# Three PSUM banks each for two kinds of score tiles in the first attention of a two-layer block

## The chip, the cores and the metric

The kernel runs on one core of a Trainium2 chip. A core has a matrix engine (TensorE, PE in the profile, with its weight loads as PEld), a vector engine (DVE), a scalar engine (ACT), a general engine (GpSimd, POOL) and SyncE (SP), which here issues the DMA transfers. Each engine works through its own instructions in order; semaphores tie them together. Matrix products are written to PSUM[...].

The metric is the device time of one execution in microseconds (us).

## The reference

Two layers run over x, 16 sequences of 256 tokens with 128 features. Each layer normalises, scales and shifts by a modulation, applies a mixing block, adds its gated output, and does the same with a second block. The change touches the first block alone: full attention with 16 heads of 8 features.

```python
q = (hidden_states @ Wq.T + bq).reshape(b, s, HEADS, HEAD_DIM)
k = (hidden_states @ Wk.T + bk).reshape(b, s, HEADS, HEAD_DIM)
v = (hidden_states @ Wv.T + bv).reshape(b, s, HEADS, HEAD_DIM)
q = q * SCALE
scores = jnp.einsum('bqhd,bkhd->bhqk', q, k)
probs = jax.nn.softmax(scores.astype(jnp.float32), axis=-1)
out = jnp.einsum('bhqk,bkhd->bqhd', probs, v).reshape(b, s, d)
return out @ Wo.T + bo
```

The blocks after it are a six-deep local transformer (attention in windows of 32 tokens and a gated feed-forward), a state-space scan, and a linear layer with a low-rank correction.

## The kernel before, in words

The whole program is one launch: `full_attention`, then `local_transformer`, then `state_space` (L1343 to L1362). Activations stay in SBUF as `xT`, features on the partitions.

`full_attention` (L132) works on groups `g` of two sequences and on units `u` of one sequence. Scores are computed twice. The first time (`scores`, L272, tile `s`, queries on the partitions) they serve only to find each row's maximum: `maxima` (L290) reduces them on DVE (L296). `turn` (L298) transposes the negated maxima (`pm`), copies them (`nT`), and writes them by DMA (L311) into spare rows of the query tile `qm`, with a row of ones in the key tile `kT`. The second time (`exponents`, L314, tile `sT`, keys on the partitions) the product so contains score minus maximum; `exponentials` (L334) apply exp on ACT (L337) into `e`; `gather` (L353) multiplies with the values into `po`, with the row sums beside them (L370). `after` (L379) inverts the sums (`pr`, reciprocal on DVE, product on POOL) and applies the output projection (`py`).

A head group has 32 rows, so the array holds four row groups. `pair(k, h)` (L340) handles two of them. For step `k + 6` it issues the first scores of row groups 2h and 2h+1, for step `k` the exponents of the other two row groups, then the second half of the first scores, then the two maxima and the two exponentials. Every `s` and every `sT` tile is [128, 2, 256] f32.

The order on each engine is written out: the loop at L417 over `k` runs under `manual_schedule` and calls `pair(k, 0)`, a slot, half of `gather(k - 1)`, a slot, `pair(k, 1)`, the other half of `gather(k - 1)`, a slot. A slot takes one piece of other work from a list `todo`: the next group's load, normalisation and projections (`before`, L197, with `xin`, `px`, the transposes at L119, called `ln2` in the code, `pq`, `qm`, `pk`), the values (`pv`), `turn` and `after`. For `k` from -6 to -1 there are first scores only; for `k` from 58 on, exponents and gather only.

PSUM is divided into tile pools. Those of the first attention:

```python
sp = ctx.enter_context(tc.tile_pool(name="a0S", bufs=2, space=PSUM))
tp = ctx.enter_context(tc.tile_pool(name="a0T", bufs=4, space=PSUM))
ps = ctx.enter_context(tc.tile_pool(name="a0p", bufs=1, space=PSUM))
op = ctx.enter_context(tc.tile_pool(name="a0o", bufs=1, space=PSUM))
```

A pool hands out its buffers in turn; the first write to a tile waits until the buffer's previous tile has been read. `scores` takes its two `s` tiles at once (L279), when it issues the first halves. `exponents` takes one `sT` after the other (L323). All pieces of other work share the one buffer of `ps`; `po` has the one of `op`. Pools of the later stages are opened after this function has closed its own.

## Time and profile before

| | |
|---|---|
| Median of 3 runs | 4388.13 us (4386.72 to 4397.31) |
| Profiled execution, its own time | 4388.87 us |
| Its span, first to last instruction | 4386.8 us |
| Busy: PE, DVE, ACT, POOL | 94%, 79%, 58%, 59% |
| First attention, first `s` to last `gather` | about 35 to 473 us |
| Local transformer | about 523 to 3815 us |
| Mean of one reduction of `s` (L296) | 688 ns |
| Mean of one exponential (L337) | 595 ns |

Each row of the order of time gives the start in us from the start of the span, the length of the merged row in us, engine, line, operation, output and inputs, shapes and count; in brackets stands the idle time of that engine before it and who ended it. In a row of waits stand the waiting engine and line, the one waited for, then us in total, times, and the longest. A matrix product in f32 appears as two records, each with its own weight load. PE's rows overlap, since products of different row groups run side by side.

### The profile page before, as it was taken

Reading aid. Unit: us, or ns where it says so; the run is one execution under the profiler, and the core shown is the slowest. Engines: PE = TensorE matmul, PEld = TensorE weight load, DVE = VectorE, ACT = ScalarE, POOL = GpSimd, SP = SyncE. Lnnn points to the kernel's source line nnn. Section 1 sums busy time; section 2 is a strip of 40 time slices with the busy share of each in tenths; the row PEclk is TensorE's granted clock in tenths of the full one; section 3 lists DMA queues with packets and bytes.
Section 4 is the critical chain, followed back from the end, with each engine's and each line's share of the span. In section 5 each row is a group of like instructions: output and inputs, shape, how many; then the busy total and the mean of one; then the engine's idle time right before and its main releaser. Section 6 shows DMA issues by size and latency. Waiting matters only on the chain.

```text
span 4386.8 us, 97989 instructions
## 1 busy us (share of the span) xinstructions
PE 4104.9 (94%) x42544; PEld 2447.8 (56%) x42544; DVE 3481.1 (79%) x4876; ACT 2527.3 (58%) x3299; POOL 2568.6 (59%) x1552
## 2 busy tenths in 40 slices
PE   6888589999999999999999999999999999779998
PEld 4444355665656656556566565565655556445554
DVE  3554488888888888888888888888888988569997
ACT  2454455555555555555555555555555555379995
POOL 1111276666666666666666666666666666258887
PEclk9999799999999999999999999999999999989999
DMA  0000100000000000000000000000000000033433
GB/s 19 7 7 4 54 2 2 2 2 22 7 1 2 2 22 6 2 2 2 22 6 2 1 2 22 6 2 1 2 1 2 2 1 2 12 98 104 115 104 85
DMA packets 59562, 83.01 MB, mean 19 GB/s; under 512 B 5800, under 2 KB 31228, under 8 KB 58364
## 3 DMA queue, kind: packets, MB, share of 16 engines
q1 hardware_dynamic: 59132, 76.74, 6.2%
q8 instruction: 335, 5.49, 0.5%
q14 instruction: 95, 0.78, 0.1%
HBM read 73.84 MB, written 2.62 MB: 17 GB/s over the span
## 4 chain that ended last, share of the span: by engine, by line
PE 57%; DVE 24%; ACT 4%; issue 2%; POOL 1%; SPq 0%; ACTq 0%; DVEq 0%; POOLq 0%; DMA 0%
PE pq L566 13%; PE py L743 11%; PE pa L724 10%; DVE w L589 4%; DVE u L578 4%; PE fp L807 4%; ACT sq L573 3%; PE fy L829 3%; PE s L669 3%; PE pt L629 3%; PE y L1241 3%; DVE ss L600 3%; PE db L1225 2%; DVE s L1231 2%; DVE pp L687 1%
## 5 line engine op out<-in xcount | busy, mean ns | idle before, releaser
L606 POOL TENSOR_TENSOR u<-u,w 128x1024 f32<-128x1024 f32 x384 | 902.0, 2360 | 321.1 <-DVE w L589 182.1
L620 POOL TENSOR_TENSOR u<-u,r 128x1024 f32<-128x1024 f32 x384 | 720.3, 1902 | 175.9 <-DVE r L616 175.9
L573 ACT ACTIVATE sq<-pq 128x1024 f32<-128x1024 f32 x384 | 388.4, 1024 | 664.8 <-PE pq L566 331.1
L706 POOL TENSOR_TENSOR pp<-pp,sm 128x1024 f32<-128x1024 f32 x192 | 367.1, 1912 | 619.1 <-DVE sm L702 619.1
L566 PE MATMUL pq<-wqk,F 128*128 128x512 f32 x1536 | 722.4, 598 | 4.0 <-ACT sq L573 1.4
L743 PE MATMUL py<-at,wvo 128*128 128x256 f32 x3072 | 712.2, 382 | 2.3 <-ACT at L734 2.3
L724 PE MATMUL pa<-pT,xw 32*128 32x512 f32 x3072 | 651.6, 616 | 30.3 <-ACT sq L573 29.2
L743 PEld LDWEIGHTS py<-at,wvo 128*128 128x128 f32 x3072 | 568.3, 190 | 134.2 <-issue 47.6
L578 DVE TENSOR_TENSOR u<-pq,cosl 128x1024 f32<-128x1024 f32 x384 | 463.2, 1206 | 190.5 <-ACT sq L573 190.5
L589 DVE TENSOR_TENSOR w<-pq,sinl 128x512 f32<-128x512 f32 x768 | 491.3, 681 | 80.5 <-PE pq L566 80.1
L734 ACT COPY at<-pa 128x1024 f32<-128x1024 f32 x384 | 383.4, 1012 | 275.3 <-PE pa L724 272.4
L600 DVE TENSOR_REDUCE ss<-sq 128x16 f32<-128x1024 f32 x384 | 455.8, 1198 | 2.6 <-ACT sq L573 1.1
L566 PEld LDWEIGHTS pq<-wqk,F 128*128 128x128 f32 x1536 | 273.5, 191 | 275.9 <-issue 244.8
L629 PEld LDWEIGHTS pt<-ident,u 128*128 128x128 f32 x3072 | 348.4, 142 | 123.9 <-issue 73.7
L629 PE MATMUL pt<-ident,u 128*128 128x128 f32 x3072 | 398.2, 275 | 20.5 <-POOL u L620 19.7
L724 PEld LDWEIGHTS pa<-pT,xw 32*128 32x128 f32 x3072 | 233.0, 184 | 291.0 <-issue 182.3
L1231 DVE TENSOR_TENSOR_SCAN s<-da,db 128x512 f32<-128x512 f32 x256 | 301.1, 1208 | 24.3 <-PE db L1225 9.9
L296 DVE TENSOR_REDUCE mx<-s 128x2 f32<-128x512 f32 x256 | 165.2, 688 | 194.0 <-PE sT L324 170.0
L807 PE MATMUL fp<-hT,w 128*128 128x512 f32 (+1 forms) x576 | 268.1, 602 | 39.8 <-DVE w L589 38.0
L669 PEld LDWEIGHTS s<-kT,qT 64*32 64x32 f32 x24576 | 254.1, 105 | 82.1 <-issue 81.1
L669 PE MATMUL s<-kT,qT 64*32 64x64 f32 x24576 | 285.1, 225 | 0.5 <-ACT kT L637 0.5
L1241 PE MATMUL y<-hc,ident 128*128 128x512 f32 x512 | 244.2, 604 | 16.1 <-POOL hc L1235 14.3
(214 smaller groups left out, 6291.1 us busy)
## 6 DMA issues: line engine op xcount, KB each, us to landing
btd<-bc SPq DMA_DIRECT2D x72, 512.0 KB
bte<-bc SPq DMA_DIRECT2D x56, 256.0 KB
wqk<-in_Wqk SPq DMA_DIRECT2D x6, 1024.0 KB
wv<-in_LWvT SPq DMA_DIRECT2D x6, 512.0 KB
wo<-in_Wo SPq DMA_DIRECT2D x6, 512.0 KB
xin<-in_x SPq DMA_DIRECT2D x8, 256.0 KB
out<-ot SPq DMA_DIRECT2D x8, 256.0 KB
w<-in_W SPq DMA_DIRECT2D x6, 341.0 KB
```

The lines of the kernel that those rows point to most:

```text
L566: nc.tensor.matmul(q.p[:, x], self.F[:, g.b0 + b, o : o + P], g.l.wqk[:, k, x, :], start=True, stop=True)
L573: self.c.nc.scalar.activation(q.sq, q.p, AF.Square)
L578: self.c.nc.vector.tensor_tensor(q.u.rearrange("p h x d -> p x h d"), q.p, g.l.cosl[:, t, k].unsqueeze(2).to_broadcast([P, 2, HEADS, DH // ...
L589: self.c.nc.vector.tensor_tensor(q.w[:, :, x], q.p[:, 1 - x], g.l.sinl[:, t, k, x, :].unsqueeze(1).to_broadcast([P, HEADS, DH // 2]), ALU. ...
L600: self.c.nc.vector.tensor_reduce(g.ss[b][:, t, k, :], q.sq.rearrange("p x h d -> p h x d"), AX.XY, ALU.add)
L606: self.c.nc.gpsimd.tensor_tensor(q.u, q.u, q.w, ALU.add)
L620: self.c.nc.gpsimd.tensor_tensor(uf, uf, g.r[b][:, t, k, :].unsqueeze(2).to_broadcast([P, HEADS, DH]), ALU.mult)
L629: self.c.nc.tensor.transpose(q.pt[:, j, :], uf[:, j * P : (j + 1) * P], self.c.ident)
L669: nc.tensor.matmul(s[qs, e, j, :], qT[es, j, qs], kT[es, j, ks : ks + 2 * W], start=False, stop=True, skip_group_check=True,)
L724: self.c.nc.tensor.matmul(pa[:, x, :], g.xw[b, t][qs, k, :], g.pT[b, t][qs, k, :], start=(k == 0), stop=(k == 1),)
L743: self.c.nc.tensor.matmul(g.py[b], g.l.wvo[:, h, :], self.at[:, h, :], start=(h == 0), stop=(h == HEADS - 1),)
L807: self.c.nc.tensor.matmul(p[0:n, x, :], g.l.w1[:, w : w + n], g.hT, start=True, stop=True)
```

## The change

The pool of the first scores `s` gets three buffers instead of two, that of the transposed scores `sT` three instead of four. Nothing else differs: the same instructions stand in the same order on every engine.

```diff
-        sp = ctx.enter_context(tc.tile_pool(name="a0S", bufs=2, space=PSUM))
-        tp = ctx.enter_context(tc.tile_pool(name="a0T", bufs=4, space=PSUM))
+        sp = ctx.enter_context(tc.tile_pool(name="a0S", bufs=3, space=PSUM))
+        tp = ctx.enter_context(tc.tile_pool(name="a0T", bufs=3, space=PSUM))
```

## The prediction

> **What bounds the kernel now.** I read the page first: TensorE is busy 94% of a span of 4386.8 us, and the chain of work that ended last does not reach back before the end of the first attention (about 473 us). So that stage was read from its own views. The busy time by stage says how long it is (columns: length, busy us of PE, its weight loads, DVE, ACT, POOL, granted clock, DMA share, GB/s):

> ```profile
> 30.00:93.00 63.00, 51.09 (x188) 29.43 (x188) 23.24 (x43) 14.65 (x24) 4.16 (x5) 1.00 0.00 1
> 93.00:446.00 353.00, 301.69 (x2589) 157.67 (x2588) 179.40 (x299) 174.49 (x327) 52.00 (x57) 0.97 0.02 6
> 446.00:473.00 27.00, 25.50 (x185) 8.86 (x184) 1.76 (x1) 15.23 (x29) 2.71 (x3) 1.00 0.00 1
> ```

> No engine is full: DVE and ACT are half idle, and PE stands still for 51 of 353 us. The waits from 93 to 446 us say for whom (us in total, times, longest):

> ```profile
> PEld s L282 <- DVE mx L296: 61.9, 119, 0.8
> ...
> PE s L282 <- DVE mx L296: 15.2, 53, 0.3
> PE py L395 <- POOL o L390: 15.0, 14, 1.1
> ```

> The first scores `s` wait for their bank to be read by the maxima. The order of time shows how one step (a pair of `s` tiles, which I call pair) runs (start, length, engine):

> ```profile
> 208.77 1.08 PE L282 MATMUL s<-kT,qm 32*128 32x256 f32 x3 [0.27 <-DVE mx L296]
> ...
> 209.37 0.18 PEld L282 LDWEIGHTS s<-kT,qm 32*128 32x128 f32 x1 [0.30 <-DVE mx L296]
> ...
> 210.43 0.64 PE L370 MATMUL po<-e,vp 128*32 128x256 f32 x8
> 210.53 1.08 ACT L337 ACTIVATE e<-sT 128x512 f32<-128x512 f32 x2 [1.51 <-PE sT L324]
> 210.62 1.29 DVE L296 TENSOR_REDUCE mx<-s 128x2 f32<-128x512 f32 x2 [0.82 <-PE sT L324]
> ...
> 211.37 1.08 PE L282 MATMUL s<-kT,qm 32*128 32x256 f32 x3 [0.29 <-DVE mx L296]
> 211.97 0.18 PEld L282 LDWEIGHTS s<-kT,qm 32*128 32x128 f32 x1 [0.31 <-DVE mx L296]
> ```

> Call X the start of a pair's second `s` (209.37). From it `gather` starts at X+1.06, the exponentials at X+1.16, the maxima at X+1.25. One reduction takes 0.69 us, the two 1.29. The next first `s` starts at 211.37, 0.06 after the first reduction has ended (210.62+0.69), the next second `s` at 211.97, 0.06 after the second. So a pair takes X to X = 1.25+1.29+0.06 = 2.60 us. It is a circle through PE, DVE and one bank each, in which neither engine is full.

> [...] the trace does not show banks, but its waits fit one bank for each tile. [...] here four row groups run side by side and the reader sets the pace, as above. [...] the clock is 0.51 from 178.9 to 182.3 us after an idle of 2.48 us.

> **The change part by part.** Nothing is added to or removed from any engine; only who waits for whom.

> *Three banks for `s`.* A pair takes two of three, in turn: (0,1), (2,0), (1,2). Its first `s` falls on the second bank of the pair before last, long free. Its second `s` falls on the first bank of the pair before, read after the first reduction. So X to X becomes 1.25+0.69+0.06 = 2.00 us, 0.60 less. PE could go at X+1.06+0.48 (gather: eight records, four side by side, two deep at 0.24) = X+1.54, so the bank still sets the pace; DVE is busy 1.29 of 2.00.

> This is won only where both `s` wait. The view has that 53 times from 93 to 446 us. From 38 to 90 us the order of time shows 8 more such pairs (2.85 us each, since weight loads take 0.28 there instead of 0.18, though the stage's clock is given as 1.00; the stagger of 0.60 is the same); two others there are followed by transposes that wait for POOL. 61 in all. Pairs with other work between them wait for something else and give nothing:

> - `pr`, `py`, `pm`, `pv`: fixed chains from X. The reciprocal starts after the second reduction (X+2.46), 1.75, then 1.27 on POOL, and `py` starts at X+5.67; then `pm`, ACT's copy, `pv`. Nothing there waits for an `s` bank alone.
> - `pq`, three ACT copies, one DVE copy, `pk`: PE idle 2.48, six times; fixed.
> - `px`, six times, one pair after a waiting one: it waits for its transfer.

> ```profile
> 198.24 2.27 SPq L311 DMA_DIRECT2D qm<-nT  x4
> ...
> 200.63 0.37 SPq L202 DMA_DIRECT2D xin<-in_x  x1
> ...
> 203.31 0.42 PEld L210 LDWEIGHTS px<-ident,xin 128*128 128x128 f32 x4 [0.58 <-DMA xin<-in_x]
> ```

> SP issues it only after four `nT` transfers, which start when ACT's copy ends; it lands 5.1 us after that copy whatever PE does. A pair that ends 0.60 earlier only makes `px` wait longer. So 6 of the 61 give nothing: 55 x 0.60 = 33.0. Where DVE's four statistics follow the reductions (0.86 us, end X+3.32), the next reduction is wanted at X+3.25: minus 0.07, six times = -0.4. At 90.6 us one pair has PE free 0.3 before its bank: +0.3. The pair after `px` waits for the second reduction alone and starts 0.2 sooner (6 x 0.2 = 1.2); that after the `ln2` transposes 0.38 sooner, of which the wait of `pq` for `hT` leaves 0.3 (6 x 0.3 = 1.8). Sum: 35.9.

> *Three banks for `sT` instead of four.* This adds a wait: the second `sT` of a pair takes the bank of the first `sT` of the pair before, read by its first exponential. In a plain pair that ends at X+1.16+0.60, +0.06 = X+1.82. The `sT` stands in PE's order behind the second `s`, at X+2.00 now. So it is covered, by 0.18. If that cover were gone, the second half of `s`, `gather`, and so both the maxima and the exponentials behind it would start later by what ACT is late. In the fixed chains the next pair comes at X+2.5 or later. ACT's other copies (0.37 to 0.59 each) mostly run after the exponentials of their pair or are done before the next. I take 0; bounds: no gain is possible from fewer banks, and the loss is at most 0.3 for each of the 55 (PE waiting for both exponentials, X+2.25+0.06 = 2.31), 17 us.

> At the end (446 to 473 us) there are `sT` and `gather` alone, one pair in 1.63 us:

> ```profile
> 454.81 1.13 PE L324 MATMUL sT<-qm,kT 32*128 32x512 f32 x4
> ...
> 455.97 1.08 ACT L337 ACTIVATE e<-sT 128x512 f32<-128x512 f32 x2 [0.54 <-PE sT L324]
> ...
> 456.44 1.13 PE L324 MATMUL sT<-qm,kT 32*128 32x512 f32 x4
> ```

> There the bank is free at 1.16+0.60+0.06 = 1.82: 0.19 lost in each of 7 pairs without other work: 1.3.

> Sum: 35.9-1.3 = 34.6 us. Everything after moves along: SP waits at 452.77 to 473.03 us for the last `gather` before it loads the next stage's weights. Against the profiled execution, 4388.9 (span 4386.8 and 2.1 around it), that is 4354.3; this execution lies 0.7 over the median of 4388.1, so 4353.5 in the median.

> **Not in the sum: the clock.** Six times the idle before `pk` costs half speed: `pk` to the next `s` takes 1.69 instead of 1.05 (as `pq` does), and the maxima come at X+2.20 instead of 1.25, together 1.6. These come 51.2 us apart, now 15 windows of 3.41; with groups of some 47 us they fall elsewhere in the window. From none avoided (0) to all (-9.5 us)[...]. I take 0 and keep both.

> **The rivals.**
> 1. *Some idle falls clear of the window* (the clock above): 4344. [...] Against: the same idle, six of six now.
> 2. *`sT` takes the place of `s`*: PE waits for both exponentials, 0.3 instead of 0.6 a pair: 4353.5+17 = 4370. For: a cover of only 0.18. Against: ACT idles 1.51 before its pair.
> 3. *It does not do what it says*: both tiles are asked for together at L279, and if their release came together, the second reduction would still bind: 4388. Against: now each `s` waits for its own reduction, 0.60 apart.
> 4. *Slower: the clock stays low.* Before 90 us weight loads take 0.28, and a pair with `sT` 3.55. If the new waits left PE so after a dip, a pair would take 2.20+0.69+0.06 = 2.95 instead of 2.60. At half speed in all 47 pairs from 93 us on that is +16: 4404. It ends slower once over 63% of these pairs run so (0.60/(0.60+0.35)). Against: only 3.4 of every 51 us are slow now, and between dips PE's idle share falls.

> **How the numbers follow.** Main case 0.63 (4345 to 4362 by itself, with the clock partly either way); rival 1 0.14; rival 2 0.12; no change 0.07; slower 0.04. The range goes from rival 1 to rival 2: 4341 to 4371; it leaves out the last two and the ends. A measurement tells about 0.3% (13 us) from no change: faster is the first three, 0.89; same 0.07; slower 0.04.

> **What would show it.** In the profile after: waiting pairs 2.00 us apart; `s` waiting for the maxima only at its second tile, with the first directly after `gather`; the total of that wait far under 61.9; `px` waiting 0.6 us longer for its transfer each time; `py` behind POOL as before; `sT` waits for `e` of 0.2 in the last 27 us only. It would be wrong if ACT's copies come ahead of the exponentials in plain pairs, if DVE is late for its reductions, or if half-clock windows grow in number.

## The result, and the profile after

The changed kernel takes 4353.61 us (median of 4 runs, 4348.96 to 4357.83), the kernel before 4390.65 us (4 runs, 4386.72 to 4397.31). The ratio is 0.9914, with a 95% interval of 0.9897 to 0.9931: 37.0 us less. The forecast was 4353.5 us, 34.6 us less.

The profiled execution shows where the gain lies. It took 4348.96 us, with a span of 4346.9 us. The last `gather` of the first attention ends at 432.56 us instead of 472.97 us, 40.4 us sooner. What follows takes 3914.3 us instead of 3913.8 us. So all of the gain is in the stage of the change, and nothing was gained or lost behind it in these two executions.

The busy time by stage of the changed kernel (columns as before: length, busy us of PE, its weight loads, DVE, ACT, POOL, granted clock, DMA share, GB/s):

```profile
30.00:88.00 58.00, 47.55 (x186) 24.93 (x186) 23.11 (x42) 14.43 (x24) 4.16 (x5) 1.00 0.00 1
88.00:413.00 325.00, 283.92 (x2644) 156.03 (x2640) 179.97 (x300) 179.52 (x337) 52.71 (x58) 0.98 0.02 7
```

The 1.00 of the first row is not a measured clock. The trace has no clock record before 88.29 us (90.11 us in the kernel before), where it notes the step to full speed, and the view counts a stretch without a record as 1.00. Most single records of `s` take 0.63 us before that time (84 of the 124 from 30 to 86 us) and 0.37 after it (76 of the 104 from 93 to 130 us); in the kernel `all_slots` below, whose trace has a record of half clock from 67.11 to 84.18 us, they take 0.63 there too. So, by the length of these records, the kernels of all twelve profiles run at half clock from the first `s` to some 84 to 93 us, apart from one window in two of them.

From 88 us on, PE stands still for 41 of 325 us, where it was 51 of 353. DVE has the same 180 us of work in a shorter stage. The waits from 87 to 418 us (us in total, times, longest) say what became of the wait for the maxima:

```profile
DVE mx L296 <- PE sT L324: 126.7, 93, 3.8
...
PEld s L282 <- issue: 31.4, 77, 1.2
...
PE py L395 <- POOL o L390: 15.0, 14, 1.1
PEld px L210 <- DMA xin<-in_x: 7.4, 6, 1.5
PEld s L282 <- DVE mx L296: 6.6, 15, 0.8
```

`s` behind the maxima was 61.9 us and is 6.6. `py` behind POOL is what it was, 15.0. The wait for the transfer of `xin` has become longer: 7.4 us in six times, where the same view of the kernel before, from 93 to 446 us, has 3.4. The order of time shows two plain pairs, the second with `px` behind it (start, length, engine):

```profile
185.06 0.64 PE L370 MATMUL po<-e,vp 128*32 128x256 f32 x8
185.16 1.08 ACT L337 ACTIVATE e<-sT 128x512 f32<-128x512 f32 x2 [0.69 <-PE sT L324]
185.24 1.29 DVE L296 TENSOR_REDUCE mx<-s 128x2 f32<-128x512 f32 x2 [1.89 <-PE sT L324]
185.63 0.55 PEld L282 LDWEIGHTS s<-kT,qm 32*128 32x128 f32 x3 [0.41 <-issue]
...
186.01 0.27 PEld L282 LDWEIGHTS s<-kT,qm 32*128 32x128 f32 x2
...
187.06 0.64 PE L370 MATMUL po<-e,vp 128*32 128x256 f32 x8
187.22 1.09 ACT L337 ACTIVATE e<-sT 128x512 f32<-128x512 f32 x2 [0.97 <-PE sT L324]
187.24 1.29 DVE L296 TENSOR_REDUCE mx<-s 128x2 f32<-128x512 f32 x2 [0.71 <-PE sT L324]
188.50 0.66 PE L210 MATMUL px<-ident,xin 128*128 128x128 f32 x4 [0.81 <-DMA xin<-in_x]
```

The maxima start at 185.24 and 187.24: 2.00 us apart, where the kernel before had 2.60. The first `s` loads its weights at 185.63, while `gather` ends, and waits for no reader. The first reduction of the pair ends near 185.93 (185.24+0.69), and the second `s` follows it near 186.00. That wait still sets the pace, but the view of waits puts it down almost nowhere, since `PEld` loads other weights meanwhile. Here a wait that sets the pace hardly appears as idle time of the engine that waits.

From one pair of maxima to the next, a group of 16 pairs (two sequences) reads so, from 88 us on; "px" and "pk" mark the step that has these pieces in it, and the values are starts subtracted from each other:

```
before  2.66 2.60 2.60 2.89 3.84 3.18 2.60 2.60(px)  2.66 2.60 2.60 2.89 3.84 3.18 2.60 7.92(pk)   51.2
after   2.07 2.00 2.00 2.89 3.84 3.18 2.00 3.06(px)  2.07 2.00 2.00 2.89 3.84 3.18 2.23 6.42(pk)   45.6
                                            mean of six                     6.42, or 7.42 to 7.80
```

Steps with a fixed chain (2.89, 3.84, 3.18) stayed to the hundredth. Seven plain steps of each group lost 0.59 or 0.60.

### The profile page after: what moved, and what is told of

Same layout as the page of the kernel before. It is cut to its first block, busy times and chain, and to the rows that moved or that the text cites. A ratio compares the mean times of both kernels' runs of the same rounds, so it can differ in the third digit from the quotient of the medians.

```text
span 4346.9 us, 97974 instructions
## 1 busy us (share of the span) xinstructions
PE 4077.9 (94%) x42544; PEld 2439.6 (56%) x42544; DVE 3482.2 (80%) x4876; ACT 2527.4 (58%) x3299; POOL 2568.6 (59%) x1552
## 4 chain that ended last, share of the span: by engine, by line
PE 58%; DVE 24%; ACT 4%; issue 2%; POOL 1%; DMA 0%; ACTq 0%; DVEq 0%; POOLq 0%; SPq 0%
PE pq L566 13%; PE py L743 11%; PE pa L724 10%; DVE w L589 4%; DVE u L578 4%; PE fp L807 4%; ACT sq L573 3%; PE fy L829 3%; PE y L1241 3%; PE s L669 3%; PE pt L629 3%; DVE ss L600 3%; PE db L1225 2%; DVE s L1231 2%; DVE pp L687 1%
## 5 line engine op out<-in xcount | busy, mean ns | idle before, releaser
L606 POOL TENSOR_TENSOR u<-u,w 128x1024 f32<-128x1024 f32 x384 | 901.9, 2359 | 321.6 <-DVE w L589 182.3
L724 PEld LDWEIGHTS pa<-pT,xw 32*128 32x128 f32 x3072 | 233.0, 184 | 291.0 <-issue 182.3
L296 DVE TENSOR_REDUCE mx<-s 128x2 f32<-128x512 f32 x256 | 165.7, 688 | 150.7 <-PE sT L324 131.5
```

The lines of the kernel that those rows point to most:

```text
L606: self.c.nc.gpsimd.tensor_tensor(q.u, q.u, q.w, ALU.add)
L724: self.c.nc.tensor.matmul(pa[:, x, :], g.xw[b, t][qs, k, :], g.pT[b, t][qs, k, :], start=(k == 0), stop=(k == 1),)
```

## Experiments

A second profile of the changed kernel came first, for the runs beside it.

> The changed kernel once more. Theory (the bank of `s` set the pace of 61 pairs, 55 of them gain 0.60 us, and about half of the half-clock windows fall away): 33 to 42 us under the kernel before, pairs 2.00 us apart. How many half-clock windows appear differs from run to run (three of six groups in the first profile), each worth about 1.4 us.

Measured: 4353.41 us (4350.07 to 4357.49), ratio 0.9907 [0.9893, 0.9922]. The profile has the same steps, with half-clock windows in the same three groups; the last `gather` ends at 432.45 us. But its span is 4354.1 us, 7.2 more than the first. I come back to that below.

**Which of the two pools matters.** One kernel takes the bank from `sT` and gives it to nobody. All diffs from here on are against the changed kernel, unless said otherwise:

```diff
-        sp = ctx.enter_context(tc.tile_pool(name="a0S", bufs=3, space=PSUM))
+        sp = ctx.enter_context(tc.tile_pool(name="a0S", bufs=2, space=PSUM))
```

> One part alone: three banks for `sT`, two for `s` (seven banks in use). Theory: plain pairs stay at 2.60 us, the pace of the second reduction; `sT` is then covered by 2.60-1.82 = 0.78; only the end of the stage loses, 0.6 us; time within 2 us of before. Rival (the bank taken from `sT` costs in the whole stage too, and the gain of `s` is larger than it looks): 5 to 17 us slower than before.

Measured: 4390.58 us (4385.36 to 4395.83), ratio 0.9992 [0.9985, 0.9998]. Order of time of this kernel, DVE alone:

```profile
184.68 1.29 DVE L296 TENSOR_REDUCE mx<-s 128x2 f32<-128x512 f32 x2 [1.38 <-PE sT L324]
187.28 1.29 DVE L296 TENSOR_REDUCE mx<-s 128x2 f32<-128x512 f32 x2 [1.30 <-PE sT L324]
```

The pairs are 2.60 us apart, as before. The fourth `sT` bank was worth nothing at that pace, and all of the gain belongs to the third `s` bank. Only the end of the stage lost, as expected: from the last maxima to the last `gather` it takes 28.79 us, as in the changed kernel, where the kernel before has 28.18.

The other kernel takes one more from `sT`, to see what a wait for the exponentials costs when it does bind:

```diff
-        tp = ctx.enter_context(tc.tile_pool(name="a0T", bufs=3, space=PSUM))
+        tp = ctx.enter_context(tc.tile_pool(name="a0T", bufs=2, space=PSUM))
```

> Three banks for `s` as after, but two for `sT`: tests the cover of 0.18 us. Theory: the second `sT` then waits for the second exponential, X+2.25+0.06 = 2.31, so plain pairs go from 2.00 to about 2.3 us (55 x 0.3 = 17 us), and the end of the stage loses some 4 more: 4370 to 4376. Rival (exponentials are far from binding, the bank count of `sT` has no weight): pairs stay at 2.00 and the time within 3 us of after.

Measured: 4366.94 us (4363.69 to 4368.16), ratio 0.9937 [0.9922, 0.9951], 13.5 over the changed kernel where 16 to 22 were expected. Its order of time:

```profile
176.25 1.29 DVE L296 TENSOR_REDUCE mx<-s 128x2 f32<-128x512 f32 x2 [0.71 <-PE sT L324]
178.50 1.29 DVE L296 TENSOR_REDUCE mx<-s 128x2 f32<-128x512 f32 x2 [0.96 <-PE sT L324]
```

This step is 2.25 us, near the 2.31 of rival 2, but not all are. The seven plain steps of a group read 2.53, 2.00, 2.25 and 2.25 between the step with `pk` (at full clock) and that with `px`, and 2.25, 2.07 and 2.18 behind `px`, 15.53 us in sum where the changed kernel has 14.14. A pair that is put off by the exponentials of the pair before gives the one after it more time, which then finds its bank free sooner. So rival 2's mechanism exists, but costs 0.20 a step instead of 0.31; and with three `sT` banks it isn't reached, since the plain steps of the changed kernel are at 2.00. The last `gather` is 12.9 us later than in the changed kernel. Of this the end of the stage took 2.1 where 4 was expected, and some 2, by an estimate, are the clock: the trace has half clock for 17.1 us of the stage from 100 us on, where the changed kernel has 10.2.

**Is it the reduction that sets the pace?** Here the maxima read half of the keys, so that a reduction is shorter and everything else is as in the changed kernel:

```diff
-                nc.vector.tensor_reduce(tops[u][:, t, jj : jj + 2, r], s, AX.X, ALU.max, negate=True)
+                nc.vector.tensor_reduce(tops[u][:, t, jj : jj + 2, r], s[:, :, 0:P], AX.X, ALU.max, negate=True)
```

> After, with maxima over half of the keys only (the other half of the first scores is left out of the maximum): a reduction takes about 0.36 instead of 0.69 us. Theory (the reduction is part of the circle, `sT` next in line): the bank of `s` would allow 1.25+0.36+0.06 = 1.67 us, the bank of `sT` 1.82 in every other pair, since a pair delayed by `sT` puts off the next one as well: 1.67 and 1.82 in turn, mean 1.75. 49 to 55 pairs x 0.25 = 12 to 14 us, and up to 0.2 us in each of 16 reciprocal chains: 12 to 17 us under after. Rival (PE sets the pace at 2.00 now): pairs stay at 2.00 us, time within 3 us of after.

Measured: 4333.52 us (4331.13 to 4342.52), ratio 0.9866 [0.985, 0.9881]; 20 us under the changed kernel. Order of time:

```profile
177.74 0.76 DVE L296 TENSOR_REDUCE mx<-s 128x2 f32<-128x256 f32 x2 [2.42 <-PE sT L324]
179.51 0.76 DVE L296 TENSOR_REDUCE mx<-s 128x2 f32<-128x256 f32 x2 [1.01 <-PE sT L324]
```

The pair took 0.53 us less on DVE, and the steps fell from 2.00 to between 1.73 and 1.80 us, though DVE had been idle a third of each. So one reduction does stand in the circle of the changed kernel. The gain is over the 12 to 17 us expected for the circle alone. In the traces the last `gather` is 18.2 us sooner (414.41 us); between 88 us and that end this execution shows a granted clock of 1.00, while the changed kernel has three half-clock windows there, and those make up some 3.5 us (the three steps with `pk` that are over 6.42). What is left, 14.7, is within the expected.

**The hand-over to `px`.** The load of `xin` is issued when the group is put on the list, which is ahead of the four `nT` transfers. The second kernel has the same edit on the kernel before:

```diff
-        def before(g, q):
...
+        def fetch(g):
+            xin = sb.tile([P, G * NT, D], F32, tag="xin", name="xin")
...
+        def before(g, q, xin):
...
-                    todo.append(before(g, made[g]))
+                    todo.append(before(g, made[g], fetch(g)))
```

> After, with the load of `xin` issued when the group is put on the list, ahead of the four `nT` transfers on SP. Theory (six pairs handed their gain to this transfer): the step with `px` takes X+1.06+0.48+0.59 = 2.13 us instead of 2.84 to 3.27 (mean 3.06), 6 x 0.93 = 5.6 us; 4345 to 4351, with some spread from the half-clock windows. Rival (`px` is late for another reason, such as PE's own queue or the shared bank): that step stays near 3.06 and the time within 2 us of after.

> The same early load of `xin`, with the banks of before (two and four). Theory: there the second reduction bound that step anyway (2.60 us with the transfer 0.2 to 0.3 late and hidden), so the early load gives 0 to 1 us against before. Rival (the transfer always cost its wait): 3 to 6 us faster than before.

Measured: 4348.93 us (4347.61 to 4352.54), ratio 0.9908 [0.9893, 0.9923], with the new banks; 4389.05 us, ratio 0.9997 [0.9989, 1.0006], with two and four. In the first, the step with `px` is 2.23 us in all six groups, where the changed kernel has 3.06 on average, and no wait for the transfer is left. With the old banks the step stays at 2.60: the same late transfer was covered by the slower pairs. So the change moved the limit of these six steps from the bank to the transfer. Six times 0.83 is 5.0, yet the last `gather` is only 2.4 us sooner (430.19 us). The clock took the rest: four of the steps with `pk` (7.12 to 8.31 us) fall into half-clock windows instead of three, and one of them into two. With the steps after them they lose 6.5 us against full clock, where the changed kernel loses 3.6. The busy time by stage of this kernel where two windows follow each other:

```profile
240.00:270.00 30.00, 24.91 (x211) 12.87 (x209) 15.21 (x21) 15.99 (x29) 3.66 (x4) 0.89 0.03 10
```

**The idle before `pk`, and the clock.** One more empty slot between `pq` and `pk` lets a pair run while the copies of `qm` are made:

```diff
             yield
+            yield
             pk = ps.tile([P, G, S], F32, tag="mm", name="pk")
```

> After, with one slot more between `pq` and `pk`, so that a pair runs while ACT and DVE make `qm`. Theory: PE's idle before `pk` falls from 2.48 to about 1.1 us, the half-clock windows inside the stage disappear, and each group is a pair (2.0 us) shorter: 6 x 2.05 = 12.3 us, and about 3.5 us from the three windows that after still has; 4335 to 4341. Rival (the maxima of that pair, which stand behind the `qm` copy on DVE, put the wait elsewhere): under 5 us faster than after; or (the half clock has nothing to do with this idle) windows of half clock remain.

Measured: 4334.43 us (4331.34 to 4341.13), ratio 0.9877 [0.986, 0.9893], 19 us under the changed kernel. In the order of time PE waits 0.84 us before `pk` instead of 2.48:

```profile
163.17 1.13 PE L248 MATMUL pk<-hT,w 128*128 128x512 f32 x2 [0.84 <-DVE qm L242]
```

From 100 us to the end of the stage there is no half-clock window left. The step with `pq` and the next one, which now has `pk` in it, take 3.97+2.45 = 6.42 us together. In the changed kernel `pq` and `pk` stand in one step, which takes with the next 6.42+2.07 = 8.49 where the clock is full and 9.6 to 9.9 where it isn't: 2.07 saved three times and 3.2 to 3.5 three times, 16.0 in sum. The last `gather` came 15.7 us sooner (416.83 us).

**Together.** The early load, the slot before `pk`, and one more slot before `py`:

```diff
             yield
             yield
+            yield
             py = ps.tile([P, S], F32, tag="mm", name="py")
```

> After, with the early load, the extra slot before `pk`, and one slot more before `py`, so that a pair runs during the product on POOL. Theory: the gains add, 5.6 + 15.8, and at `py` each of 15 units saves the idle of 1.07 us and somewhat more, 15 x 1.2 = 18: 4311 to 4320. Rival (with these waits gone the shared bank of the other work or ACT becomes the bound): 4325 to 4335.

Measured: 4326.16 us (4324.69 to 4329.0), ratio 0.9856 [0.9841, 0.987]. This is faster than each part alone, and still it is 6 us over the upper end of what the sum gave. In the stage most of the gain is there: the last `gather` ends at 400.25 us, 32.3 before that of the changed kernel, where the sum asked for 33.5 to 42.5. The groups of instructions from 87 to 418 us show PE's idle before `py` at 3.3 us, where the kernel with the slot for `pk` alone has 15.9 (L400 is L395 of the changed kernel; line, engine, output and inputs, shapes, count, then busy us, mean ns, and the idle before with what ended it):

```profile
L400 PE MATMUL py<-o,wo 128*128 128x256 f32 x64 | 19.0, 422 | 3.3 <-POOL o L394 3.3
```

The rest of what is missing came later: after the last `gather` this execution took 3922.8 us instead of 3914.3. The second profile of the changed kernel has 3921.6 there, and the kernel with two `s` and three `sT` banks 3922.5. Set side by side, instruction by instruction, these three fall behind the first profile at the same places. The first is near 584 us of the changed kernel (0.9 us in two of them; some 5 in `all_slots`, which had been 3.9 ahead there). At 3413 us each loses 1.7 us more, near 3747 us another 1.7; some more steps follow in the state-space stage after 3770 us. At 3413 us, the busy time of one window in the first profile of the changed kernel:

```profile
3396.00:3407.00 11.00, 10.11 (x164) 6.32 (x161) 10.89 (x16) 4.95 (x5) 5.64 (x4) 1.00 0.01 1
```

and of the same window in its second profile:

```profile
3396.00:3407.00 11.00, 10.12 (x157) 5.09 (x154) 10.90 (x15) 4.95 (x5) 4.94 (x4) 0.84 0.01 1
```

The same stretch runs at a mean clock of 1.00 and of 0.84. If PE's work follows the clock, 0.16 of these 11 us, 1.8 us, is lost; that is an estimate from the two clocks, and the step is 1.7. Over all profiles the length behind the last `gather` goes with the clock: the seven with 125 to 129 us of half clock there took 3913.8 to 3915.3 us, the five with 136 to 150 us took 3918.8 to 3922.8. Whether the longer part in `all_slots` was chance or came from the spread steps, two more runs were to tell; the second leaves out the slot before `py`.

> The same kernel as all_slots once more, to place the 8 us by which that run's gain fell short. There its last gather ended at 400.25 us, 32.3 before that of the changed kernel, as the sum had it, but what comes after the last gather took 3922.8 us instead of 3914.3; the second profile of the changed kernel shows 3921.6 there as well, with two steps of about 1.7 us and one of about 4.5 us between 3400 and 3850 us. Theory A (the later part falls into one of two lengths, run by run, whatever the edit): last gather again at 400 +- 1, and some executions near 400 + 3914 + 2 = 4316 us, others near 4325. Theory B (the spread steps themselves cost it, for good): last gather at 400 and all executions at 4324 to 4330.

> all_slots without the extra step ahead of py: the early load of x and the extra step ahead of pk alone. If the gains add by their place in the order: px pairs 2.23 instead of about 3.2 in six groups, 5.8 us off spread_pk's last gather at 416.8, so 411 us, and no half-clock window before pk; total 411 + 3914 to 3923 + 2 = 4327 to 4336 us. The rest of all_slots, 411 - 400 = 11 us, is then the py step's. If the early load only calls up half-clock windows, as in early_x, where the clock fell in more windows than after: last gather at 414 to 417.

Measured: 4324.35 us (4322.98 to 4325.1), ratio 0.9847 [0.9833, 0.9862], for the first; 4329.8 us (4327.49 to 4331.64), ratio 0.9861 [0.9844, 0.9878], for the second. The second is as the sum had it: last `gather` at 412.3 us (411 expected), and 3914.2 us behind it. For the first, neither theory came out whole. Its last `gather` ended at 404.25 us, 4.0 later than in the run before it. Of these, 2.4 are there by 90 us, and there the run before it was at full clock from 63.69 to 67.11 us and from 84.18 us on, this one only from 87.75 us on; 1.4 come from one step of 4.12 instead of 2.72 us near 122 us, where this trace has a half-clock window from 121.88 us and the other has none. The later part took 3918.8 us, 4.0 less, with 136 us of half clock instead of 150. No execution came near 4316 us. So the lengths of both parts vary between executions of one kernel, here by 4 us each, and in both the granted clock differed with them. Why the half-clock windows behind the stage fall as they do, and why all eight executions of this kernel lie between 4323 and 4329 us, stays open.

The slot before `py` gave less than expected. In the groups where both kernels are at full clock one takes 41.53 us with it and 42.80 without (the kernel with the early load and the slot before `pk`): 0.64 a unit instead of 1.2.

## Why the prediction was right or wrong

- *The circle of a pair.* Right at full clock: 2.60 became 2.00 us, by 1.25+0.69+0.06. That one reduction stays in it is shown by the kernel with shorter maxima, and that the third bank of `s` breaks the old circle by the kernel that only takes one from `sT`. Before the first `gather` the sum came out (its end moved from 90.14 to 84.90, 5.2 us, where 8 x 0.60 is 4.8), but not by its terms. The stretch is at half clock there, by the 0.63 us of its `s` records, which the prediction saw in its weight loads and could not explain from the 1.00 of the view. Six steps of first scores alone went from 2.85 to 2.02, 0.83 each instead of 0.60, and a seventh won 0.39; the three with `sT` in them won 0.60 each, to 2.95 in the end, the half-clock figure of rival 4; and three steps with other work gave 1.7 back. That these nearly cancel is luck; why the 0.60 became 0.83 was not followed.
- *Fixed chains give nothing.* Right: `py`, `pm` and `pv` steps at 2.89, 3.84 and 3.18 us in both, and 15.0 us of `py` behind POOL in both.
- *Six pairs handed to `px`.* Right. The step went from 2.60 to 3.06 us; 0.60 more, less the 0.2 that the pair after it was to win, is 3.00. The transposes' step (`ln2`) lost 0.37 where 0.30 was put down.
- *Three banks for `sT` cost nothing in plain pairs.* Right, since they run at 2.00. The cover of 0.18 is not shown to be exact; that a wait appears once it is gone is shown with two banks.
- *The tail, 1.3 us.* Sign right, size wrong. The step that failed is "0.19 lost in each of 7 pairs without other work". The order of time after, ACT alone, start and length:

```profile
410.07 1.09 ACT L337 ACTIVATE e<-sT 128x512 f32<-128x512 f32 x2 [0.68 <-PE sT L324]
411.76 1.08 ACT L337 ACTIVATE e<-sT 128x512 f32<-128x512 f32 x2 [0.60 <-PE sT L324]
413.50 1.08 ACT L337 ACTIVATE e<-sT 128x512 f32<-128x512 f32 x2 [0.66 <-PE sT L324]
```

The exponentials start 1.69 and 1.74 us apart, not 1.82; before it was 1.63 on average. They alternate, so the mean delay of these is 0.09. The formula took the delay of each pair against an undelayed one before it. The tail lost 0.61 us instead of 1.3, and just as much in the kernel that only takes a bank from `sT`.

- *The clock, taken as 0.* This is the term that was off. The half-clock windows of the stage fell from six to three, so rival 1 came half true. The half-clock windows of the stage are 3.41 us long in both traces. The 2.48 us of idle before `pk` was followed by one six times of six before and three times of six after. The order of time of the changed kernel has both kinds, one with the slow clock:

```profile
165.86 1.18 PE L247 MATMUL pk<-hT,w 128*128 128x512 f32 x2 [2.48 <-DVE qm L242]
166.97 0.79 PE L282 MATMUL s<-kT,qm 32*128 32x256 f32 x2
166.98 1.22 PE L324 MATMUL sT<-qm,kT 32*128 32x512 f32 x2
...
212.66 1.13 PE L247 MATMUL pk<-hT,w 128*128 128x512 f32 x2 [2.48 <-DVE qm L242]
213.71 0.48 PE L282 MATMUL s<-kT,qm 32*128 32x256 f32 x2
213.72 0.70 PE L324 MATMUL sT<-qm,kT 32*128 32x512 f32 x2
```

Two `s` records take 0.79 and 0.48 us, two `sT` records 1.22 and 0.70. What tells them apart in this trace is where the idle lies. All changes of the clock on record in the traces before and after stand on a grid of 3.41 us: from the step to full speed on, full and half clock in turn last 78.51, 3.41, 88.75, 3.41, 88.75, 3.41 and 81.92 us in the changed kernel, which is 23, 1, 26, 1, 26, 1 and 24 times 3.413; in the kernel before, 37.55 us and then 3.41 and 47.79 in turn, which is 11, 1 and 14 times. The busy time by window of this grid, the window with the idle and the one after it, for the first and then for the second:

```profile
163.38:166.79 3.41, 0.93 (x2) 0.30 (x2) 0.81 (x1) 1.57 (x3) 0.00 (x0) 1.00 0.00 0
166.79:170.20 3.41, 3.41 (x25) 1.59 (x28) 1.03 (x2) 2.53 (x4) 0.00 (x0) 0.50 0.00 0
211.17:214.58 3.41, 1.93 (x14) 0.99 (x14) 0.81 (x1) 1.34 (x3) 0.00 (x0) 1.00 0.02 5
214.58:217.99 3.41, 3.41 (x40) 1.80 (x38) 2.25 (x4) 2.70 (x6) 0.00 (x0) 1.00 0.00 0
```

The first idle lies whole in one window, and PE is busy for 0.93 us of it; the second (from 210.17 us) is cut by the edge at 211.17, and PE is busy for 1.93 us. In the kernel before, all six idles lie whole in one window (2.48 us) and are followed by half clock; in the changed kernel three do, and the three that are cut, with 1.30, 1.49 and 1.66 us on their longer side, are not. Eight of the profiles have this idle in each of six groups, 48 in all. The 29 of them that put 1.91 us or more into one window were followed by half clock in the next; the 19 that put at most 1.77 us into either were not. So rival 1, that some idle falls clear of the window, asked the right question, and in these traces the count of half-clock windows goes with where the groups fall on the grid; what links the two is not shown. In the kernel before, an idle came every 51.2 us, 15 windows, and kept its place, 0.56 to 0.83 us behind an edge; in the changed kernel two groups together take some 92.3 us, close to 27 windows (92.2), so that every second idle is cut. Even six of six was not sure at the old pace: the kernels with two `s` banks and either three `sT` banks or the early load each have one such idle without half clock.

The step with `pk` was 7.92 us and is 6.42 in three groups and 7.42 to 7.80 in the others: 3 x 1.50 + 3 x 0.35 = 5.5 us.

The balance of the stage: the predicted 35.9 without the tail, less the 0.6 that the tail lost, plus 5.5 for the clock, is 40.8; the last `gather` came 40.4 us sooner. Against the profiled execution the forecast was 4354.3 us and the time 4348.96, 5.3 less, which is the clock. That the median came so close to 4353.5 us is partly luck: the three other executions took 3.8 to 8.9 us longer than the profiled one, probably in the later part, where the second profile shows 7.3 more. Their mean clocks on record, 0.983, 0.982 and 0.981 against 0.984, fit this, but they were not profiled, so it is argued.

- *The rivals.* "It does not do what it says" and "slower, the clock stays low" have fallen: the total of the wait is 6.6 us, and the clock is low less often. "`sT` takes the place of `s`" needs one `sT` bank less than the change leaves.

## What to carry to other kernels

Where two tiles in turn go through a producer and a slower reader, each with its own bank, look whether the circle holds the sum of both reads, as it did here; one bank more staggered them, and only one read stayed in the circle. Follow the circle for one step and name what is next within 0.2 us, because the pairs with other work in them are handed to it at once (here a transfer that had been covered). Then work a delay through two steps before multiplying it: what was put off in one step was here often no longer in the way of the next (0.20 for 0.31, 0.09 for 0.19).
